# Router scores of four token tiles in one product, with the router's weights stationary and the tokens moving

## The chip, the core and the metric

The kernel runs on one core of one Trainium2 chip. A core has five engines that work in parallel, each through its own queue of instructions in order: PE (TensorE, matrix products), DVE (VectorE), ACT (ScalarE), POOL (GpSimd) and SP (SyncE, here only for issuing transfers). Products land in PSUM, which has eight banks; everything else lies in SBUF. The metric is the device time of one execution in microseconds (us), and the time of a kernel is the median of its runs.

## The reference

The input is x, 4 batches of 512 tokens with 512 features. A conditioning stage makes hidden rows, and a mixture of 32 experts is applied to them: each token goes to the four experts with the highest router scores, each expert takes at most C = 512 tokens, and what comes later is dropped. Cut to what matters:

```
q_emb  = relu(cond @ W3 + b3)                              # per batch
hidden = relu(((n*x + sum_over_tokens(x)) * q_emb) @ W2 + b2)
h      = rmsnorm(hidden) * norm_w
scores = softmax(h @ gate_w.T)                             # 2048 tokens x 32 experts
w, ids = top_k(scores, 4);  w = w / sum(w)
# place of a token in its expert = number of earlier (token, expert) pairs of the same expert
routed = sum over the four experts of  w * (silu(g) * u) @ w2[e],  g, u = split(h @ w13[e])
shared = (silu(h @ shared_gate) * (h @ shared_up)) @ shared_down
out    = x + hidden + routed + shared
```

All of it is in f32.

## The kernel before

The 2048 tokens are 16 tiles of 128 (NT = 16); four tiles make a batch of the input and also a group for the router's bookkeeping (TB = 4). The kernel has three stages. The first, the token stage, takes the tiles one after another and ends with a table that says which token stands in which slot of which expert. The second is a loop over blocks of expert work, which gathers rows, multiplies them with the weights of two experts at once (in two column tiles of PE, 64 columns each) and scatters the results. The third sums up. The change is in the first.

Each step t of the loop at L818 writes instructions for several tiles at different points of their way. The order in which the calls stand in the code is the order in each engine's queue; semaphores are derived from reads and writes, cell by cell in SBUF and by whole bank in PSUM. The calls of one step are, in order:

- `hidden(t)` (L591): four products of 128x512 into a bank D (PE); DVE adds b2; ACT applies relu, the square with its sum, and the root.
- `logits(t - 2)` (L641): router scores of one tile. The tile's tokens, hT of 128x128 per chunk of features, are the stationary operand, and the router's weights gateT (128x32 per chunk) move. The bank is TX[1] or TA[1] in turn.
- `prefix(g)` (L695): five small products that count earlier pairs, in step i = 1 of a group.
- `h_transpose(t - 1)` (L629): PE turns h of the tile before into bank TA[0], ACT copies it to hT (DVE in the last step).
- `slots` (L793): products of one-hots, two tiles in each of steps i = 0 and i = 1 of the group after.
- `top4(t - 2)` (L648): DVE takes the maximum of a tile's scores, subtracts it, and ranks them (max, max_index).
- `first`: one piece of the group's bookkeeping, given by i: `taken`, `places`, `one_hots`, `one_hots`.
- `normed(t)` (L608): DVE takes the reciprocal and makes h; SP sends h to DRAM.
- `rest`: the second piece of the same: `totals`, `places2`, and `one_hots` of another tile.
- For i = 1, 2 of a batch: `z_mean` (ACT) and `z_finish` (POOL) for the next batch's input z, two chunks of features per step.
- `transfers`: larger loads, among them `load_xt(2)` at t = 4 and `load_xt(3)` at t = 8, which fill the z of batches 2 and 3. They stand in SP's queue behind that step's h.

Group and step come from `g, i = divmod(t - 5, TB)` (L820), so the group of tiles 0 to 3 has its `taken` at t = 5. In `one_hots` (L789) the place one-hots are made by ACT for even tiles and by DVE for odd ones, four per tile; the block one-hots (L780) are four DVE instructions of 128x128 per tile. Group 2 has only i = 0 and 1 in the loop; the rest of it and group 3 follow after the loop (from L908 on), in an order written out by hand, together with the shared expert's first products, the tables, and the first gathers.

Of the kernel before, what the change touches and what calls it, by code (L numbers as in the profile page):

```python
# [6 lines left out]
F32 = mybir.dt.float32  # L7
# [4 lines left out]
ALU = mybir.AluOpType  # L12
AX = mybir.AxisListType

P = 128
EPS = 1e-6

LEAST_EXPONENT = -87.33655
# [6 lines left out]
class Program:  # L25
# [87 lines left out]
    def op(self, eng, fn, r=(), w=(), lane=None, signal=True, also=(), key=None):  # L113
        need = {}

        def depend(token):
            key, val = token
            need[key] = max(need.get(key, 0), val)

        for token in also:  # L120
            depend(token)
        for x in r:
            for c in self.cells(x):
                if c in self.writer:
                    t = self.writer[c]
                    if not (eng == "PE" and self.owner[t[0]] == "PE"):
                        depend(t)
        for x in w:
            for c in self.cells(x):
                if c in self.writer:  # L130
                    t = self.writer[c]
                    if not (eng == "PE" and self.owner[t[0]] == "PE"):
                        depend(t)
                for t in self.readers.get(c, {}).items():
                    if not (eng == "PE" and self.owner[t[0]] == "PE"):
                        depend(t)
        if lane is not None:
            ring = self.lanes[lane]
            key = ring[self.lane_next[lane]]
            self.lane_next[lane] = (self.lane_next[lane] + 1) % len(ring)  # L140
            if self.count[key]:
                depend((key, self.count[key]))
            self.count[key] += 16
            token, step = (key, self.count[key]), 16
        elif signal:
            key = key or self.own[eng]
            self.count[key] += 1
            token, step = (key, self.count[key]), 1
        else:
            token, step = None, 0  # L150
        waits = self.learn(eng, need)
        if token:
            self.seen[token] = dict(self.known[eng])
            for x in r:
                for c in self.cells(x):
                    self.readers.setdefault(c, {})[token[0]] = token[1]
            for x in w:
                for c in self.cells(x):
                    self.writer[c] = token
                    self.readers.pop(c, None)  # L160
        else:
            assert not w
        self.out[eng].append((waits, fn, token and token[0], step))
        return token
# [43 lines left out]
def adaln_moe_kernel(nc, stack, x, xt, cond, W3, b3, W2, b2, norm_w, gate_w, wx, sg, su, sd, out):  # L208
    B, S, H = x.shape
    Q = cond.shape[1]  # L210
    E = gate_w.shape[0]
# [4 lines left out]
    NT = T // P  # L216
    TB = S // P
    HC = H // P
# [22 lines left out]
    op = k.op  # L241
# [10 lines left out]
    def keep(name, shape, dtype):  # L252
        n = SIZE[dtype]
        for s in shape[1:]:
            n *= s
        t = k.sbuf(name, shape, dtype, top[0])
        top[0] += -(-n // 32) * 32
        return t

    hid0 = keep("hid0", [P, TB, H], F32)  # L260
    hT = [keep(f"hT{b}", [P, HC, S], F32) for b in range(B)]
    ident = keep("ident", [P, P], F32)
# [4 lines left out]
    xT = [keep(f"xT{i}", [P, HC, P], F32) for i in range(2)]  # L267
# [7 lines left out]
    last = keep("last", [P, 2, NCOL], F32)  # L275
# [10 lines left out]
    gateT = keep("gateT", [P, HC, E], F32)  # L286
# [4 lines left out]
    iota_lo = keep("iota_lo", [P, P], F16)  # L291
    iota_bk = keep("iota_bk", [P, 2, NCOL], F16)
    tok = keep("tok", [P, NT], F32)
# [12 lines left out]
    lg = keep("lg", [P, NT, E], F32)  # L306
    topv = keep("topv", [P, NT, 8], F32)
    topr = [keep(f"topr{i}", [P, 8], F32) for i in range(2)]
# [3 lines left out]
    GROUPS = [(t, t + TB) for t in range(0, NT, TB)]  # L312
# [60 lines left out]
    def instead(name, shape, dtype, of):  # L373
        return k.sbuf(name, shape, dtype, k.place[of.name][1])
# [3 lines left out]
    kept = instead("kept", [P, NT, E], F32, rows[2])  # L378
    W3_sb = instead("W3_sb", [P, QC, H], F32, eo[0])
    sq = instead("sq", [P, H], F32, eo[2])  # L380
    within = instead("within", [P, NT, E], F16, eo[3])


# [11 lines left out]
    TX = [k.bank(f"TX{i}", i) for i in range(2)]  # L395
    GU = [k.bank(f"GU{i}", 2 + i) for i in range(2)]
    TA = [k.bank(f"TA{i}", 4 + i) for i in range(2)]
# [99 lines left out]
    def dve_scalar(o, i, s1, s2, *ops):  # L497
        op("DVE", lambda e: e.tensor_scalar(o, i, s1, s2, *ops), r=[i], w=[o])
# [39 lines left out]
    def transposes(pairs):  # L538
        def fn(e):
            for o, i, n in pairs:  # L540
                last = e.transpose(o, i, ident[:n, :n])  # L541
            return last
        return fn
# [27 lines left out]
    for c in range(QC):  # L571
        op("PE", transposes([(TA[0][:, c * 8 : c * 8 + B], cond_sb[:, c * P : (c + 1) * P], B)]),
           r=[cond_sb[:], ident[:]], w=[TA[0][:]])
# [4 lines left out]
    for c in range(HC):  # L578
        bank = (TX + GU)[c]
        op("PE", matmuls([(bank[:, 0:B], W3_sb[:, kc, c * P : (c + 1) * P], condT[:, kc, :]) for kc in range(QC)]),  # L580
           r=[W3_sb[:], condT[:]], w=[bank[:]])
# [59 lines left out]
    def logits(t):  # L641
        b, j = divmod(t, TB)
        bank = logit_bank(t)
        pl = bank[:, 0:E]
        op("PE", matmuls([(pl, hT[b][:, c, j * P : (j + 1) * P], gateT[:, c, :]) for c in range(HC)]),
           r=[("hT", t), gateT[:]], w=[bank[:]])

    def top4(t):  # L648
        bank = logit_bank(t)
        pl = bank[:, 0:E]  # L650
        l, tr = lg[:, t, :], topr[t % 2][:]

        op("DVE", lambda e: e.max(tr, pl), r=[bank[:]], w=[tr])
        op("DVE", lambda e: e.tensor_scalar(l, pl, tr[:, 0:1], LEAST_EXPONENT, ALU.subtract, ALU.max),
           r=[bank[:], tr], w=[l])
        tv, ti = topv[:, t, :], ids[:, t, :]
        op("DVE", lambda e: e.max(tv, l), r=[l], w=[tv])
        op("DVE", lambda e: e.max_index(ti, tv, l), r=[l, tv], w=[ti])


    def count(o, i):
# [118 lines left out]
    def block_hots(g, t):  # L780

        i = t - GROUPS[g][0]
        e1, bh = ej[g % 2][:, i, :], blh[t % 4]
        for n in range(K):
            op("DVE", lambda e, n=n: e.tensor_scalar(bh[:, n, :], iota_lo[:], e1[:, n : n + 1], tok[:, t : t + 1],
                                                     ALU.is_equal, ALU.mult),
               r=[iota_lo[:], e1, tok[:]], w=[bh[:, n, :]])

# [4 lines left out]
    def slots(t):  # L793

        lh, bh = loh[t % 4], blh[t % 4]

        def fn(e):
            for n in range(K):
                last = e.matmul(GU[1][:, 0:P], lhsT=bh[:, n, :], rhs=lh[:, n, :], start=(t == 0 and n == 0),
                                stop=(t == NT - 1 and n == K - 1))  # L800
            return last
        op("PE", fn, r=[lh[:], bh[:]], w=[GU[1][:]])
# [14 lines left out]
                 13: lambda: fetch(4)}  # L817
    for t in range(NT):  # L818

        g, i = divmod(t - 5, TB)  # L820
        first, rest = [], []
        if g in (0, 1) or g == 2 and i < 2:
            u = GROUPS[g][0] + 2 * (i - 2)
            first, rest = [([lambda: taken(g)], [lambda: totals(g)]),
                           ([lambda: places(g)], [lambda: places2(g)]),
                           ([lambda: one_hots(g, u)], [lambda: one_hots(g, u + 1)]),
                           ([lambda: one_hots(g, u)], [lambda: one_hots(g, u + 1)])][i]
        hidden(t)
        if t == 1:
            gate_transpose()  # L830
        if t >= 2:
            logits(t - 2)
        if g in (0, 1, 2) and i == 1:
            prefix(g)
        if t >= 1:
            h_transpose(t - 1, "ACT" if t < NT - 1 else "DVE")
        if g in (1, 2) and i in (0, 1):
            for u in (0, 1):
                slots(GROUPS[g - 1][0] + 2 * i + u)

        if t >= 2:
            top4(t - 2)
        for fn in first:
            fn()
        normed(t)
        for fn in rest:
            fn()
        if t == 0:
            constants()
        b, i = divmod(t, TB)  # L850
        if b + 1 < B and i in (1, 2):
            for c in (2 * i - 2, 2 * i - 1):
                z_mean(b + 1, c)
                z_finish(b + 1, c)
        if t >= TB:
            sum_rows(t)
        if t in transfers:
            transfers[t]()
# [55 lines left out]
    for e in range(FREE):  # L914
# [22 lines left out]
       r=[cumj[:], ones[:]], w=[TA[1][:]])  # L937
# [6 lines left out]
       w=[active[:]])  # L944
# [4 lines left out]
       r=[ranks[:], before[:], till[:], active[:]], w=[TA[1][:]])  # L949
    op("PE", matmuls([(TA[0][0:1, 4 * NCOL : 4 * NCOL + E], active[:, i : i + 1], upto[:]) for i in range(2)]),  # L950
       r=[active[:], upto[:]], w=[TA[0][:]])
# [13 lines left out]
    for i in range(2):  # L965
        op("DVE", lambda e, i=i: e.tensor_scalar(place[i][:], iota_bk[:], rank[:, i : i + 1], None, ALU.is_equal),
           r=[iota_bk[:], rank[:]], w=[place[i][:]])
    op("DVE", lambda e: e.tensor_tensor(places12[:], place[0][:], place[1][:], ALU.add), r=[place[0][:], place[1][:]],
       w=[places12[:]])
    for t in (12, 13):  # L970
# [9 lines left out]
       r=[scol[:], units], w=[TA[0][:]])  # L980
    op("PE", lambda e: e.matmul(TA[0][0:1, 2 * NCOL : 4 * NCOL], lhsT=ecol[:], rhs=units, start=True, stop=True),
       r=[ecol[:], units], w=[TA[0][:]])
# [21 lines left out]
    for t in range(12, NT):  # L1004
# [11 lines left out]
       r=[empty[:], spare[:], GU[0][:]], w=[idxf[:]])  # L1016
# [14 lines left out]
       r=[needs[:]], w=[tab[:]])  # L1031
# [6 lines left out]
       w=[rel[:]])  # L1038
# [294 lines left out]
    for b in order:  # L1333
# [8 lines left out]
       w=[copies[:]])  # L1342
# [4 lines left out]
    for j in (1, 2, 3, 0):  # L1347
# [4 lines left out]
       r=[copies[:], lrow[0][:], lrow[1][:]], w=[GU[1][:]])  # L1352
# [89 lines left out]
```

## Time and profile before

| | |
|---|---|
| median of 3 runs | 560.28 us (560.17 to 561.66) |
| the profiled execution: its own time | 562.46 us |
| its span in the profile | 560.6 us |
| granted clock of PE over the span | 0.997 |
| PE busy | 549.7 us (98%) |
| DVE busy | 287.2 us (51%) |
| ACT busy | 220.8 us (39%) |
| POOL busy | 287.4 us (51%) |
| start of the expert loop | 121.65 us |
| 12 of the 16 router products (logits) on PE, in the chain | 0.81 us each |
| 64 block one-hots on DVE | 15.6 us busy |

The rows of the profile are times in us from the start of the span unless marked ns. An engine's busy time is a sum over the whole span and can hide that the engine is full in one stage. The chain of waits follows the work that ended last back to the start, at each step to what released it. PE's matmuls are pipelined: a row's duration runs to its last result, so two rows in a row overlap, and the spacing of their starts is what PE really needs. The product of two f32 operands appears as two records.

### The profile page before, as it was taken

To read this page: it belongs to the slowest core of one execution; us is meant where nothing else is said; L and a number is where in the kernel's file an instruction comes from. 1 tells how busy PE (TensorE), PEld (TensorE's weight loads), DVE (VectorE), ACT (ScalarE), POOL (GpSimd) and SP (SyncE) were. 2 spreads that over 40 slices of the span, in tenths; PEclk is the share of its full clock that TensorE was granted. 3 is DMA by queue.
4 is the path that set the end of the run, shared out by engine and by line. 5 is a ranking of instruction groups with operands and counts; after the bars stand their busy time and mean duration, and the time that the engine had idled before them with its cause. 6 is when DMAs were issued, how large, how long until landed. Compare 5 with 4: busy or idle time off the path is not lost.

```text
span 560.6 us, 7813 instructions
## 1 busy us (share of the span) xinstructions
PE 549.7 (98%) x2518; PEld 237.1 (42%) x2518; DVE 287.2 (51%) x807; ACT 220.8 (39%) x428; POOL 287.4 (51%) x237
## 2 busy tenths in 40 slices
PE   8999999999999999999999999999999999989997
PEld 5455665443433333433334433334333334334342
DVE  3569998956455444555444554444554445210422
ACT  3648666823334433434333344333344334300000
POOL 1102200235766666576667776756766766415800
PEclk9999999999999999999999999999999999989999
DMA  8886888956686968797997889989999655439921
GB/s 300 286 324 239 283 337 279 360 174 190 111 198 112 238 147 197 197 238 180 250 260 185 236 242 267 238 230 251 222 250 248 113 103 92 67 56 381 343 77 75
DMA packets 49198, 120.21 MB, mean 214 GB/s; under 512 B 8404, under 2 KB 9432, under 8 KB 48056
## 3 DMA queue, kind: packets, MB, share of 16 engines
q1 hardware_dynamic: 32896, 83.24, 43.9%
q0 software_dynamic: 15040, 34.39, 31.2%
q10 hardware_dynamic: 1208, 1.92, 1.0%
q8 instruction: 26, 0.43, 0.3%
q14 instruction: 28, 0.23, 0.1%
HBM read 89.36 MB, written 34.36 MB: 221 GB/s over the span
## 4 chain that ended last, share of the span: by engine, by line
PE 92%; DVE 3%; ACT 2%; issue 1%; DMA 1%; POOL 0%; SPq 0%; DVEq 0%; ACTq 0%
PE GU L1157 37%; PE D L1180 20%; PE D L548 7%; PE TX L541 5%; PE TX L548 5%; PE GU L548 4%; PE TA L541 4%; PE D L1319 2%; PE TA L1319 2%; PE TX L880 2%; PE TA L548 1%; DMA z<-in_xt_dram 1%; PE D L598 1%; PE D L558 1%; PE D L1312 1%
## 5 line engine op out<-in xcount | busy, mean ns | idle before, releaser
L1108 POOL DMA_INDIRECT y_rows<-eo,sidx x122 | 180.4, 1479 | 102.8 <-DMA y_rows<-eo,sidx 34.7
L1157 PE MATMUL GU<-ring,xT 128*64 x488 | 214.5, 592 | 0.6 <-issue 0.6
L1157 PE MATMUL GU<-up,xT 128*64 128x512 f32 x488 | 214.5, 592 | 0.0
L1157 PEld LDWEIGHTS GU<-ring,xT 128*64 128x64 f32 x488 | 66.8, 137 | 139.4 <-issue 139.4
L1165 DVE TENSOR_TENSOR act<-silu,GU 128x256 f32<-128x256 f32 x61 | 25.7, 422 | 176.3 <-ACT silu L1164 143.4
L1180 PE MATMUL D<-ring,actT 128*64 x244 | 111.3, 599 | 0.2 <-issue 0.2
L1180 PE MATMUL D<-down,actT 128*64 128x512 f32 x244 | 111.3, 599 | 0.0
L1100 POOL DMA_INDIRECT rows<-h_rows,idx x66 | 70.5, 1068 | 33.6 <-issue 13.1
L1164 ACT ACTIVATE silu<-GU 128x256 f32<-128x256 f32 x61 | 23.5, 385 | 147.6 <-PE GU L1157 147.6
L1157 PEld LDWEIGHTS GU<-up,xT 128*64 128x64 f32 x488 | 66.8, 137 | 0.0
L1068 ACT COPY up<-ring 128x1024 f32 x62 | 64.3, 1037 | 5.8 <-DVE up L1068 5.5
L1184 ACT ACTIVATE eo<-D,wrow 128x512 f32<-128x512 f32 x61 | 41.9, 687 | 51.5 <-PE D L1180 42.7
L1180 PEld LDWEIGHTS D<-ring,actT 128*64 128x64 f32 x244 | 30.9, 136 | 58.0 <-issue 58.0
L548 PE MATMUL D<-W_sb,z 128*128 128x512 f32 x120 | 54.3, 595 | 0.2 <-POOL z L563 0.2
L1068 DVE COPY up<-ring 128x1024 f32 x62 | 44.7, 721 | 0.8 <-issue 0.8
L1068 DVE COPY down<-ring 128x1024 f32 x62 | 42.7, 714 | 0.1
L1096 DVE COPY xT<-TX 128x512 f32<-128x512 f32 x62 | 40.0, 686 | 4.4 <-issue 2.0
L563 POOL TENSOR_SCALAR z<-z,vs,q_sb 128x512 f32<-128x512 f32 x12 | 9.8, 816 | 55.7 <-ACT junk L554 55.6
L541 PE MATMUL TX<-ident,rows 128*128 128x128 f32 x248 | 32.3, 273 | 0.0
L1171 ACT COPY actT<-TA 128x256 f32<-128x256 f32 x61 | 22.8, 373 | 24.1 <-PE TA L541 18.1
L548 PEld LDWEIGHTS D<-W_sb,z 128*128 128x128 f32 x120 | 21.7, 190 | 22.4 <-issue 22.0
L1180 PEld LDWEIGHTS D<-down,actT 128*64 128x64 f32 x244 | 30.9, 136 | 0.0
(207 smaller groups left out, 561.2 us busy)
## 6 DMA issues: line engine op xcount, KB each, us to landing
ring<-in_L_ffn_w_dram SPq DMA_DIRECT2D x96, 384.0 KB
ring<-in_L_ffn_w_dram SPq DMA_DIRECT2D x8, 1536.0 KB
y<-y_rows SPq DMA_DIRECT2D x8, 1024.0 KB, 13.4
h_rows<-h SPq DMA_DIRECT2D x16, 256.0 KB, 4.5
y_rows<-hid SPq DMA_DIRECT2D x16, 256.0 KB, 4.1
out_dram<-y SPq DMA_DIRECT2D x16, 256.0 KB, 2.3
z<-in_xt_dram SPq DMA_DIRECT2D x14, 256.0 KB, 5.3
y_rows<-eo,sidx POOLq DMA_INDIRECT x122
```

The costliest lines, as they stand in the source:

```text
L541: last = e.transpose(o, i, ident[:n, :n])
L548: last = e.matmul(o, lhsT=lt, rhs=rh, start=(n == 0), stop=(n == len(terms) - 1))
L1068: return e.copy(dst, src) if eng == "ACT" else e.tensor_copy(dst, src)
L1096: return op("DVE", lambda e: e.tensor_copy(xt[:], pt[:].rearrange("p (c t) -> p c t", c=HC)), r=[pt[:]], w=[xt[:]])
L1100: op("POOL", lambda e: e.indirect_dma_start(out=r[:], out_offset=None, in_=h_dram, in_offset=bass.IndirectOffsetOnAxis(ap=idx[:, i : i + 1 ...
L1108: op("POOL", lambda e, o=o, y=y, at=at: e.indirect_dma_start(out=y, out_offset=bass.IndirectOffsetOnAxis(ap=at, axis=0), in_=o, in_offset= ...
L1157: last = e.matmul(pg[h * U : (h + 1) * U, :], lhsT=xt[:, c, h * U : (h + 1) * U], rhs=w, start=(c == 0), stop=(c == HC - 1))
L1164: op("ACT", lambda e: e.activation(s, pg[:, 0:I], AF.Silu), r=[pg[:]], w=[s])
L1165: op("DVE", lambda e: e.tensor_tensor(a, s, pg[:, I : 2 * I], ALU.mult), r=[s, pg[:]], w=[a])
L1171: op("ACT", lambda e: e.copy(at[:], pt[:, 0 : IC * P].rearrange("p (c t) -> p c t", c=IC)), r=[pt[:]], w=[at[:]])
L1180: last = e.matmul(po[h * U : (h + 1) * U, :], lhsT=at[:, c, h * U : (h + 1) * U], rhs=w2, start=(c == 0), stop=(c == IC - 1))
L1184: op("ACT", lambda e: e.activation(o, po[:], AF.Copy, scale=w), r=[po[:], w], w=[o])
```

## The change

The scores of a group of four tiles are made in one go when its fourth tile is ready, at t = 5, 9 and 13. In `group_logits` the router's weights are the stationary operand, 32 columns wide, and the tokens move, 128 at a time; the four tiles of the group go to the four column tiles of PE, that is to partitions 0 to 31, 32 to 63 and so on of one bank, with the chunks of features as the outer loop. The result stands with experts in the partitions. DVE copies it to SBUF (lgT), PE turns it back (`group_back`), and DVE takes maximum, subtraction and lower bound for all four tiles at once (`group_top4`), and then ranks each tile as before (`rank_tile`). The last group keeps the old form.

The block one-hots of groups 0 and 1, eight tiles, are made by POOL instead of DVE. The bookkeeping of each group is one step later (`t - 6`). lgT lies in the place of xT[0], which is first used later.

```diff
+    lgT = instead("lgT", [P, P], F32, xT[0])
...
         op("DVE", lambda e: e.tensor_scalar(l, pl, tr[:, 0:1], LEAST_EXPONENT, ALU.subtract, ALU.max),
            r=[bank[:], tr], w=[l])
+        rank_tile(t)
+
+    def rank_tile(t):
+        l = lg[:, t, :]
         tv, ti = topv[:, t, :], ids[:, t, :]
         op("DVE", lambda e: e.max(tv, l), r=[l], w=[tv])
         op("DVE", lambda e: e.max_index(ti, tv, l), r=[l, tv], w=[ti])
+
+    def group_logits(g):
+        bank, ht = TA[1], hT[g]
+        def fn(e):
+            for c in range(HC):
+                for q in range(TB):
+                    last = e.matmul(bank[q * E : (q + 1) * E, 0:P], lhsT=gateT[:, c, :], rhs=ht[:, c, q * P : (q + 1) * P],
+                                    start=(c == 0), stop=(c == HC - 1))
+            return last
+        op("PE", fn, r=[gateT[:]] + [("hT", g * TB + q) for q in range(TB)], w=[bank[:]])
+        op("DVE", lambda e: e.tensor_copy(lgT[:], bank[:, 0:P]), r=[bank[:]], w=[lgT[:]])
+
+    def group_back():
+        op("PE", transposes([(TX[1][:, 0:P], lgT[:], P)]), r=[lgT[:], ident[:]], w=[TX[1][:]])
+
+    def group_top4(g):
+        pl = TX[1][:, 0:P].rearrange("p (t e) -> p t e", t=TB)
+        t0, t1 = GROUPS[g]
+        l, tr = lg[:, t0:t1, :], topr[g % 2][:, 0:TB]
+        op("DVE", lambda e: e.tensor_reduce(tr, pl, AX.X, ALU.max), r=[TX[1][:]], w=[tr])
+        op("DVE", lambda e: e.tensor_tensor(l, pl, tr.unsqueeze(2).to_broadcast([P, TB, E]), ALU.subtract),
+           r=[TX[1][:], tr], w=[l])
+        dve_scalar(l, l, LEAST_EXPONENT, None, ALU.max)
+        for t in range(t0, t1):
+            rank_tile(t)
...
-            op("DVE", lambda e, n=n: e.tensor_scalar(bh[:, n, :], iota_lo[:], e1[:, n : n + 1], tok[:, t : t + 1],
+            op("POOL" if g < 2 else "DVE", lambda e, n=n: e.tensor_scalar(bh[:, n, :], iota_lo[:], e1[:, n : n + 1], tok[:, t : t + 1],
                                                      ALU.is_equal, ALU.mult),
...
-        g, i = divmod(t - 5, TB)
+        g, i = divmod(t - 6, TB)
...
-        if t >= 2:
+        if t >= NT - TB + 2:
             logits(t - 2)
+        if t >= TB and t % TB == 1:
+            group_logits(t // TB - 1)
         if g in (0, 1, 2) and i == 1:
             prefix(g)
...
-        if t >= 2:
+        if t >= TB and t % TB == 1:
+            group_back()
+        if t >= NT - TB + 2:
             top4(t - 2)
+        if t >= TB and t % TB == 1:
+            group_top4(t // TB - 1)
         for fn in first:
             fn()
         normed(t)
```

## The prediction

> **What bounds the kernel now.** I read the page, then the table of stages, the chain of waits, and the timelines of DVE, ACT, POOL and PE over the first 125 us. The change touches only the token stage, which ends where the expert loop begins, at 121.6 us.
>
> ```profile
> 48.30:68.50 20.20, 20.17 (x102) 12.50 (x103) 19.47 (x76) 14.82 (x39) 3.47 (x4) 1.00 0.84 283
> 68.50:93.70 25.20, 25.18 (x130) 15.80 (x129) 22.76 (x93) 15.42 (x36) 0.00 (x0) 1.00 0.84 301
> 93.70:121.60 27.90, 26.55 (x115) 12.63 (x114) 23.27 (x84) 17.72 (x44) 10.53 (x13) 1.00 0.82 288
> 121.60:560.00 438.40, 431.89 (x2002) 169.56 (x2002) 194.22 (x461) 148.93 (x251) 265.58 (x199) 1.00 0.75 194
> ```
>
> The columns are the stretch, its length, and the busy us of PE, PEld, DVE, ACT and POOL. From 48.3 to 68.5 DVE is busy 19.47 of 20.20 us beside a PE that never stops: time taken from one is not yet time won. The expert loop is PE-bound, so it only moves with its start.
>
> ```profile
> 35.25 0.76 DVE h L611
> ...
> 36.95 5.33 DMA z<-in_xt_dram
> 42.30 0.73 ACT junk L554 x2
> ...
> 46.63 1.65 POOL z L563 x2
> 48.28 0.04 issue
> 48.33 3.70 PE D L548 x8
> 52.03 0.81 PE TX L548 x8
> 52.84 0.47 PE TA L541 x4
> ...
> 92.75 0.91 PE TA L548 x8
> 93.66 0.02 issue
> 93.68 0.21 DVE topr L653
> ```
>
> This is the chain (start, us, what). Two places matter. At 48.33 hidden(8) starts on a loaded z: the load is issued behind h(4), then come ACT's means and POOL's z_finish; PE's own work up to there is not on the chain. At 93.68 the chain passes to DVE, in top4(15); from there DVE runs almost without a gap to 112.
>
> **The change, part by part.**
>
> *PE.* Twelve logits products of 0.81 us go. Three group products and three turns back come. The nearest row to a group product is the expert loop's:
>
> ```profile
> 129.82 0.38 PE L541 MATMUL TA<-ident,act 128*128 128x128 f32 x2
> 130.43 0.64 PE L1180 MATMUL D<-ring,actT 128*64 x1 [0.23 <-issue]
> 130.44 0.64 PE L1180 MATMUL D<-down,actT 128*64 128x512 f32 x1
> 130.91 0.59 PE L1180 MATMUL D<-ring,actT 128*64 x1
> ```
>
> Two column tiles start 0.01 us apart and take 0.43 us a record of 512 columns, with two records a product: they run side by side. A 128-column product is then 2 x 0.43/4 = 0.215 us; sixteen of them take 0.86 us four abreast, 1.7 two abreast, 3.44 in a row. The same rows show an idle 0.23 us at the switch from the full array to column tiles; leaving them and the last record's tail (0.16 beyond its spacing) add about 0.35. [...] The row gives the drain its price: 0.86 + 0.23 + 0.35 = 1.45 us per group product (bounds 1.1 and 4.0). [...] The router's weights are in fact loaded for each of the four column positions; the short load (a 64-column load is 0.14 us and hides) costs nothing while the previous product streams. The turn back is a transpose, 0.11 us in a row of others, 0.25 with its wait for the lgT copy, which runs while PE turns h (0.47). If DVE is late, hidden(t+1) behind it in PE's queue is late by as much. Per group: 4 x 0.81 = 3.24 out, 1.70 in, 1.5 us won, three times 4.6.
>
> *DVE.* Four top4 took 0.95 each from start to start, 3.8. In their place: the lgT copy 0.25 (the gateT copy is 0.28), a reduction 0.31 (csum 0.36, wsum 0.28), a subtraction 0.30 (sel 0.27), a maximum 0.2 (between 0.14, a quarter of DVE's z_finish, and 0.28, within), four rankings at 0.42: 2.75. Won 1.05 per group; each of these small estimates is good to 0.1. The 32 block one-hots that leave DVE were 0.96 per tile, 7.7 us in all.
>
> *POOL.* No one-hot on POOL is in the trace. The same form is z_finish, 0.82 us for 512 f32 elements: a quarter, 0.20, is the low end, all of it the high end. iota_lo of the same shape took 0.24, a 128x128 tensor_tensor 0.43; I take 0.31. Sixteen start when places2 ends, so 5 us of POOL work stand in its queue ahead of z_finish for batch 3 (not due for 10 us) and ahead of slots two steps later. At 0.31 that is hidden; the cover is gone above 0.8.
>
> [...] The row:
>
> ```profile
> 46.98 0.55 DVE L737 SCALAR_TENSOR_TENSOR lo<-blk,ppc 128x16 f32<-128x16 f32 x1
> ...
> 46.63 1.64 POOL L563 TENSOR_SCALAR z<-z,vs,q_sb 128x512 f32<-128x512 f32 x2 [1.92 <-ACT junk L554]
> ```
>
> That DVE instruction takes 0.17 elsewhere; under POOL's it waited until the first of the two had ended. [...] Since starts fall anywhere, I take 0.4 us at the start of hidden(12); low end 0.
>
> *What moves.* Each group's steps come one tile later (t - 6). For group 2, places and places2 move from t = 14 to t = 15, ahead of h(15) and top4(14) on DVE. SP's issues keep their order.
>
> **The sum, walked step by step.** PE needs 3.44 for hidden and 0.47 to turn h.
>
> 1. To hidden(8). hidden(4) needs POOL's z_finish, which ends at 28.61: it starts at 28.65, was 28.95. So h(4), the load and everything behind it move by 0.3. PE has 1.5 us more than it needs, and waits: hidden(8) at 48.05, was 48.33. The first group's win is lost there, up to 0.3.
> 2. To hidden(12). PE: 4 x 3.91, a group product and turn back 1.70, prefix 0.22, two slots 0.45 each: 66.5. But ACT now makes the place one-hots of tile 2 (1.85 us) at t = 9, ahead of the means of batch 3. hid(9) comes at 55.65, its relu, square and root end at 58.05, hT(8) 58.55, one-hots 60.4, two means 62.1, the same of tile 10 and hT(9) 64.5, two means 66.0, z_finish 67.0. hidden(12) starts at 67.0, 67.4 with the port; it was 68.47.
> 3. To top4(15). The turn back of group 2 is at hidden(12) + 3.44 + 0.47 + 3.44 + 1.45 + 0.45 + 0.25 = +9.5. From there DVE has no gap: group_top4 2.5, h(13) 0.9, place one-hots 0.65, hid(14) 0.65, top4(12) 0.95, taken 2.0, h(14) 0.9, totals 0.5, hid(15) 0.65, a wait of 0.4 for PE's turn, hT(14) 0.6, top4(13) 0.95, places 1.6, h(15) 0.85, places2 0.85, top4(14) 0.95, block one-hots 0.95: 16.9. So top4(15) is at hidden(12) + 26.4; it was +25.2. The late shift takes 1.2 back. At 67.4 + 26.4 = 93.8 it stands at 0.1 past the old 93.68.
> 4. idf, behind it, took 0.65 instead of 0.17 to 0.29 under POOL's product of the weights; ACT's exp now comes some 0.6 earlier, so about 0.25 of that stall goes.
>
> Sum: -0.15 us on the span. From top4(15) on, DVE's work is the same and back to back, and PE follows it. The sum is made against the profiled execution (span 560.6, its own time 562.46, 1.9 outside the span); I carry the difference to the median, 560.28, which is 2.2 below that execution: 560.1. Both kernels should have the same 1.9 outside. A difference under 0.3%, 1.7 us, is about what a measurement of this kernel cannot tell from no change.
>
> **The rivals.**
>
> *The stage follows PE alone (faster).* If loads and ACT kept ahead and DVE's slack held, 4.6 us would come through, 555.7; with half of it, 558. For it: PE shows no gap from 24 to 88. Against it: the chain at 48.33 does not go through PE, and step 3 is DVE's. Chance 0.18, 555.5 to 558.6.
>
> *POOL and DVE take each other's turns (slower).* One place: from the end of places2 (50.85), while POOL works off sixteen one-hots. [...] For it: the stretched lo, and a form of one-hot that was never on POOL. Against it: DVE has about 2 us of room at t = 8. Chance 0.28; 561.9 to 566.
>
> *The product does not do what it says (slower).* If the four column tiles run in a row, 2.5 us come on top at t = 13, uncovered, and 2.1 at t = 9 (the other 0.5 hides behind z): 564.7. Against it are the two halves 0.01 us apart. Chance 0.04. Two abreast, 0.85 more each time, stays within the range.
>
> **How the numbers follow.** Likeliest, 0.50: a balance, 558.6 to 561.9, with 560.1 as its number. Faster 0.18, slower 0.28 + 0.04 = 0.32. The range 557.2 to 563.0 takes in half of each side case and leaves out about 0.2.
>
> **What would show it.** Right: hidden(8) within 0.5 us of 48.1 and waiting for z; hidden(12) near 67.4; sixteen one-hots of about 0.31 each on POOL in a row after places2; the group product near 1.45 us with its tiles starting together; top4(15) near 93.8, DVE full from group_top4 of group 2 on; expert loop from about 121.5. Wrong: the loop starting before 120 or after 123.3; hidden(12) still on a chain of PE alone; one-hots over 0.45 us, or a stretched h and place one-hots at 54 to 57; sixteen products in a row.

## The result and the profile after

| | before | after |
|---|---|---|
| median, us (7 runs each) | 560.28 (559.92 to 561.66) | 558.84 (558.28 to 559.19) |
| ratio, 95% interval | | 0.9958 [0.9938, 0.9979] |
| span of the profiled execution, its own time | 560.6, 562.46 | 557.0, 558.84 |
| hidden(4), hidden(8), hidden(12) on PE | 28.95, 48.33, 68.47 | 28.95, 48.38, 68.27 |
| top4(15) on DVE | 93.68 | 94.33 |
| start of the expert loop | 121.65 | 122.26 |
| from there to the end of the span | 438.95 | 434.74 |
| waits and products of PE right behind the loop | 2.21 + 5.40 | 0 + 3.43 |

By the medians the changed kernel is 1.4 us faster, 0.26%, inside the 0.3% that the prediction called no difference. The interval of the ratio leaves out 1, so a small gain is there. The table shows something odd: the stage that was changed ended 0.6 us *later*, and the whole gain of the two profiled executions, 3.6 us of span, lies behind the expert loop, in code that the change did not touch.

The table of stretches of the changed kernel, cut at the same events as before (the columns are again the stretch, its length, and the busy us of PE, PEld, DVE, ACT and POOL):

```profile
48.38:68.27 19.89, 18.46 (x103) 9.58 (x103) 15.72 (x58) 15.69 (x42) 16.94 (x20) 1.00 0.90 301
68.27:94.33 26.06, 24.96 (x145) 14.98 (x146) 20.11 (x85) 13.92 (x33) 13.06 (x16) 1.00 0.87 308
94.33:122.26 27.93, 26.55 (x116) 12.62 (x115) 23.30 (x85) 17.70 (x44) 10.56 (x13) 1.00 0.76 263
122.26:557.00 434.74, 429.92 (x2002) 169.06 (x2002) 193.55 (x461) 148.92 (x251) 266.31 (x199) 1.00 0.76 195
```

From hidden(8) to hidden(12) PE is busy 18.46 us instead of 20.17, and DVE 15.72 instead of 19.47: both were relieved as intended. The stretch became shorter by only 0.25 us (19.89 instead of 20.14). POOL went from 3.47 to 16.94. The chain of waits says who took the place:

```profile
35.36 0.77 DVE h L612
...
36.98 5.42 DMA z<-in_xt_dram
42.42 0.73 ACT junk L555 x2
...
49.61 0.75 DVE h L612
51.27 13.40 POOL blh L818 x16
64.68 3.54 POOL z L564 x4
68.27 3.70 PE D L549 x8
...
75.84 1.01 PE TA L672 x32
...
93.54 0.88 DVE blh L818 x4
```

hidden(8) still hangs on the same load of z. hidden(12), which was on a chain of PE's own work, now hangs on POOL: sixteen block one-hots in 13.40 us, then z_finish, which stood behind them in POOL's queue. What PE gained it spends waiting, as its list of waits shows (us in total, times, longest):

```profile
PE D L549 <- POOL z L564: 3.3, 3, 1.3
PE TA L542 <- DVE h L612: 2.9, 3, 1.3
```

The list of before had 0.2 us for z in one place and nothing for h.

Now the stretch behind the loop. First the chain of before, then that of after; in both, the first row is the last work of the loop's ending and the last row the first eight products after it:

```profile
489.70 3.63 PE TX L548 x8
493.33 2.21 issue
495.54 5.40 PE GU L548 x8
```

```profile
490.29 3.63 PE TX L549 x8
493.92 3.43 PE GU L549 x8
```

"issue" is time in which PE waited for nothing that the profile shows. Between these two places PE jumps: the kernel has one ending for each possible number of blocks (61 were run), and from each a branch goes to the common code behind them. The eight products that follow the standstill also ran slowly. The table of stretches of before has the granted clock as the third column from the right:

```profile
495.50:497.50 2.00, 1.96 (x4) 0.99 (x5) 0.00 (x0) 0.00 (x0) 0.00 (x0) 0.86 0.04 9
497.50:499.50 2.00, 2.00 (x4) 0.69 (x3) 0.00 (x0) 0.00 (x0) 0.00 (x0) 0.50 0.00 0
499.50:501.00 1.50, 1.50 (x6) 0.69 (x5) 0.00 (x0) 0.00 (x0) 0.00 (x0) 0.72 0.00 0
```

So before paid 2.21 us of standstill and 5.40 - 3.43 = 1.97 us in slow products, 4.2 in all, and after paid nothing. By the three rows the clock stood at half for about 3.4 us, from some 1.4 us behind the standstill on, which is 1.7 of the 1.97 us; the other 0.27 came at full clock too (3.70 instead of 3.43 in before_again, below). 4.2 less the stage's 0.6 is the 3.6 us between the spans. The medians differ by 1.4 only, so an ordinary execution of before must pay less than the profiled one. The experiments had to settle two things: whether the standstill has to do with the edit's work at all, and where PE's and DVE's relief went.

### The profile page after: what moved, and what is told of

Read it like the earlier page. It is cut to its first block, busy times and chain, and to the rows that moved or that the text cites. A ratio compares the mean times of both kernels' runs of the same rounds, so it can differ in the third digit from the quotient of the medians.

```text
span 557.0 us, 7816 instructions
## 1 busy us (share of the span) xinstructions
PE 543.0 (97%) x2521; PEld 228.6 (41%) x2521; DVE 276.3 (50%) x763; ACT 220.8 (40%) x428; POOL 314.6 (56%) x269
## 4 chain that ended last, share of the span: by engine, by line
PE 87%; DVE 5%; POOL 3%; ACT 3%; DMA 1%; issue 1%; SPq 0%; ACTq 0%; DVEq 0%
PE GU L1196 38%; PE D L1219 20%; PE TX L542 5%; PE D L549 4%; PE TX L549 4%; PE GU L549 4%; PE TA L542 4%; POOL blh L818 2%; PE D L1358 2%; PE TA L1358 2%; PE TX L919 1%; DMA z<-in_xt_dram 1%; PE D L599 1%; POOL z L564 1%; ACT sq L606 1%; PE D L559 1%
```

## Experiments

### Where the gain is: the place of code behind the loop

The edit puts products into PE's ending for 80 blocks, where they are never executed. Here it is with the eight products of before_tail_moved; before_tail_256 has 128 of them, and after_tail_moved, on the changed kernel, 120:

```diff
             ending(i)
+            if i == NMAX:
+                k.raw("PE", lambda e: [e.matmul(D[1][:, 0:1], lhsT=zero[:, 0:P], rhs=zero[:, 0:1], start=True, stop=True)
+                                       for _ in range(8)])
```

The expectations count two instructions for a product, and that is wrong. In the trace of before a product of f32 operands is two records, each with its own load of weights (60 products of `hidden` at L548: 120 records and 120 loads), which makes four instructions. In the compiled programs the code behind the loop moved by 32 instructions (not 16), 512 (not 256) and 480 (not 240). The edit of this case moved it by 15.

**before_tail_moved.** 

> The kernel before, with eight products that are never executed put into PE's code of the ending for 80 blocks (61 are run), so that PE's code after the expert loop lies 16 instructions further on; all executed work is the same. Theory (the gain of the change is where that code comes to lie: PE stood 2.2 us at the jump behind the expert loop and ran its next eight products in 5.4 us instead of 3.4): no wait of over 0.3 us ahead of these products, 3.4 to 3.7 us for them, expert loop from 121.7 as before, 558.0 to 558.6 us, some 0.5 under the changed kernel. Rival (the stall was an accident of one profiled execution, and the change's gain lies in its own work): 560.3 us, no different from before.

Measured: 559.04 us (22 runs) beside 560.52 of the kernel before (64 runs), ratio 0.9969 [0.9958, 0.998]: 0.4 us above the range of the theory, and clear of the rival. The chain has no standstill:

```profile
489.99 3.63 PE TX L548 x8
493.62 3.43 PE GU L548 x8
```

**before_again**, the kernel before, unchanged. 

> The kernel before, profiled a second time. Theory (its code behind the loop lies badly, and each execution pays some of it): a wait of 0.3 to 2.5 us at or near the first products after the loop, span less loop start 435.5 to 439 us (four other profiles have 434.3 to 434.8, the first one of this kernel 438.95). Rival (an accident of the first profile): no wait, 434.3 to 434.8 us. The start of the expert loop also tells how far two profiles of the same token stage differ: 121.65 the first time, 122.4 in the kernel with the code moved.

Measured: this execution took 559.89 us, its span is 558.1, the loop starts at 121.86. The standstill is there again, shorter, and without the slow products:

```profile
489.61 3.63 PE TX L548 x8
493.24 1.46 issue
494.70 3.70 PE GU L548 x8
```

**before_tail_256.** 

> The kernel before with 128 never executed products in PE's ending for 80 blocks, so that PE's code after the loop lies exactly 256 instructions further on, at the same place modulo 256. [...]

Measured: 561.48 us (12 runs), ratio to before 1.0007 [0.9989, 1.0025], no different from before, beside 559.04 of before_tail_moved. With 512 instructions instead of 32 the standstill is back, and so is the slow clock (0.93 over 480 to 500 us):

```profile
490.07 3.63 PE TX L548 x8
493.70 2.14 issue
495.84 5.40 PE GU L548 x8
```

**after_tail_moved.** 

> The changed kernel, with 120 never executed products in the same place, so that PE's code after the loop lies 240 instructions further on, within one instruction of where the kernel before had it modulo 256. Theory (place of the code): the wait of about 2 us ahead of the first eight products after the loop comes back, they take over 5 us, 560.3 to 563 us, that is 1.5 to 4 more than the changed kernel. Rival (an accident, or the gain is in the work): 558.8 us, no wait there.

Measured: 559.15 us, ratio to before 0.9974 [0.9965, 0.9984]; no standstill (493.13 3.43 directly behind 489.50 3.63). The expectation failed, but the kernel was not where it was meant to be: it lies 15 + 480 = 495 instructions past the place of before, 17 short of the 512 of before_tail_256, instead of 15 + 240 = 255. So this run does not test whether the changed kernel stands still at the place of before.

What follows: a move of 32 instructions, with every executed instruction the same, gives 1.5 us; a move of 512 gives nothing. Counted from the place of before, the standstill is there in all three profiles at 0 and 512 (before, before_again, before_tail_256), and in none of the eleven others, at 15, 32 or 495. So what counts is the place of the code. The traces show transfers of instructions there: the queue q8, which the profile lists as "instruction" and which I take for PE's, moves packets of 16 KiB, 26 in each of the three executions with a standstill against 25 in before_tail_moved and in after. In those three the packet that was under way as the standstill began landed at 494.23, 493.36 and 494.44 us, and PE went on 1.31, 1.34 and 1.40 us later; in the other eleven PE starts these products before the packet under way has landed (in after at 493.92, the packet landing at 494.29). So "issue" here fits a wait for code, whose length would follow from when a packet lands; that is my reading of these times, and no run shows it directly. The number of packets alone does not tell: after_tail_moved has 26 too. Not shown is which place of the code is the bad one and why, nor how often the effect comes back: the runs have it at 0 and 512, and that the place should count modulo 256, as two of the expectations have it, was my assumption.

The edit lengthened PE's code ahead of this point by 15 instructions, and that was enough: 558.84 and 559.15 with the change against 559.04 for before with its code moved.

With that, the stage itself: the loop starts at 121.65, 121.86, 122.39 and 122.25 in the four profiles in which the stage is that of before (mean 122.04), and at 122.26 and 121.83 in the two in which it is that of after (mean 122.05). The 0.6 us between the first two profiles is inside this scatter. The work of the change is worth nothing that can be seen, within about 0.4 us.

### Where the relief went: the parts alone

**before_hots_pool.** Edit, on before_tail_moved:

```diff
-            op("DVE", lambda e, n=n: e.tensor_scalar(bh[:, n, :], iota_lo[:], ...
+            op("POOL" if g < 2 else "DVE", lambda e, n=n: e.tensor_scalar(bh[:, n, :], iota_lo[:], ...
```

> Of the change the POOL part alone: the kernel before, with the code moved by 16 instructions as in the first experiment (its time 559.04 us is the one to compare with), and the block one-hots of the first eight tiles on POOL. Theory (DVE sets the stage, and the 7.7 us that leave it count where a group's steps pile up): expert loop 1 to 3 us earlier than with the code moved alone (122.4), 556 to 558 us. [...]

Measured: 559.35 us, beside 559.04 of before_tail_moved; the loop starts at 121.96. DVE's busy time between 68 and 94 us fell from 23.95 to 20.98, and nothing came of it: with twelve products for the logits PE is busy 25.98 of these 26 us. The theory fell. (PE also stood 1.58 us at the jump into the ending, which was 0.4 to 0.9 in the other profiles but one, where it was 1.36, so part of the 559.35 is not the stage's.)

**after_hots_dve.** Edit, on the changed kernel: the same line back to `op("DVE", ...`. 

> The changed kernel with the block one-hots of all tiles on DVE again. Theory (sixteen one-hots of 0.84 us on POOL hold up z_finish of batch 3, 1.3 us of PE's wait at hidden(12)): z_finish follows ACT's means, hidden(12) at 66.7 to 67.4 instead of 68.3, expert loop from 121.2 to 121.9 instead of 122.3, 558.0 to 558.6 us. Rival (DVE is as full as POOL: 7.7 us of one-hots in its queue delay hid and h, so that hidden(12) waits for the means instead): hidden(12) at 68.0 or later, loop from 122.3 or later, 558.8 to 560 us.

Measured: 563.02 us, ratio 1.0046 [1.0032, 1.006]; hidden(12) at 70.58, loop from 126.55. The theory fell, and the rival's price was too small. POOL's queue is empty, but DVE now holds everything up:

```profile
PE TA L542 <- DVE h L612: 4.9, 6, 1.4
PE D L549 <- POOL z L564: 2.6, 3, 1.1
```

At t = 9 a whole group's ranking, two tiles' block one-hots and one tile's place one-hots stand on DVE between hid(9), at 57.43, and hid(10), at 65.33; in the changed kernel these two are at 56.16 and 61.79. ACT's relu and means, and z_finish, follow hid(10).

**after_one_earlier.** Edit, on the changed kernel:

```diff
-        g, i = divmod(t - 6, TB)
+        g, i = divmod(t - 5, TB)
```

> The changed kernel with the groups' bookkeeping one tile earlier (t - 5 as before, instead of t - 6), one-hots still on POOL. Theory (the late shift of group 2 costs 1.2 us between hidden(12) and top4(15), and one-hots a tile earlier are off POOL before z_finish of batch 3 is due): hidden(12) near 67, top4(15) at hidden(12) + 25, expert loop from 120 to 121, 556.6 to 557.6 us. Rival (ranking and counting of a group in one step of DVE at t = 5, 9 and 13 delay h and so PE): hidden(8) or hidden(12) 1 us or more later than in the changed kernel, loop from 122.3 or later, 558.8 us or more.

Measured: 561.38 us, ratio 1.0019 [1.0009, 1.0028]; hidden(8) at 49.39, hidden(12) at 70.39, loop from 124.70. The rival was right: ranking and counting of a group fall into one step, hid(9) stands at 57.38 and hid(10) at 65.08, and PE also waits 2.9 us for mask at the prefix products:

```profile
PE TA L542 <- DVE h L612: 3.0, 5, 1.3
PE GU L549 <- DVE mask L697: 2.9, 3, 1.2
```

What follows: taking the logits together relieves PE but gives DVE the ranking of four tiles at once. With the one-hots left on DVE the loop starts 4.5 us later than in the changed kernel (126.55 against 122.05), and with the bookkeeping left a step earlier 2.65 us later (124.70). The move of the one-hots to POOL and the later step do not gain anything against the kernel before; they keep the gathered ranking from colliding with DVE's other work. The product without either move was not run.

### POOL's price for a one-hot

**after_pool_sizes.** Edit, on the changed kernel: five more tensor_scalar instructions on POOL near the start. 

> The changed kernel with five more POOL instructions at the start, where POOL is idle; their results are not used: the one-hot's form (is_equal, mult, two scalars per partition) at 512 f16 elements, at 64, at 128 with add in place of is_equal, at 128 with one operation and one scalar, and at 128 f32 elements. Theory A (POOL's price is per instruction, 0.84 us for 128 elements beside 0.82 for z_finish's 512): all five 0.75 to 0.9 us. Theory B (the price is per element, and the comparison or f16 is slow): 512 elements 2.5 to 3.4 us, 64 about 0.42, and the form with add or with f32 about 0.2 to 0.3. Theory C (the price is per operation or scalar): the one with one scalar about 0.42.

Measured (timeline of POOL, start, us, what; in the order of the list above):

```profile
2.17 2.09 POOL L546 TENSOR_SCALAR blh<-iota_lo,tok 128x512 f16<-128x512 f16 x1
4.26 0.57 POOL L546 TENSOR_SCALAR blh<-iota_lo,tok 128x64 f16<-128x64 f16 x1
4.82 0.44 POOL L546 TENSOR_SCALAR blh<-iota_lo,tok 128x128 f16<-128x128 f16 x1
5.25 0.59 POOL L546 TENSOR_SCALAR blh<-iota_lo,tok 128x128 f16<-128x128 f16 x1
5.84 0.78 POOL L546 TENSOR_SCALAR lgT<-iota_pp,tok 128x128 f32<-128x128 f32 x1
```

None of the three theories has it alone. The comparison is what is dear: with is_equal and mult the price grows by (2.09 - 0.57) / 448 = 3.4 ns per element on top of about 0.35 us; with add and mult it is 0.44 us at 128 elements and 0.79 at z_finish's 512, about 0.9 ns per element (f16 against f32, so a rough figure). f16 or f32 makes little difference (0.84 in the kernel, 0.78 here). Where I scaled 512 elements of z_finish down to 128, I had the wrong operation and left out the fixed part. This one execution took 561.47 us: its z load took 6.59 us, and hidden(8) came at 50.16.

### What the stage hangs on instead

**after_loads_early.** Edit, on the changed kernel:

```diff
-    3: lambda: fetch(0), 4: lambda: load_xt(2), 6: lambda: fetch(1), 8: lambda: load_xt(3),
+    3: lambda: (load_xt(2), fetch(0)), 6: lambda: fetch(1), 7: lambda: load_xt(3),
```

> The changed kernel with the loads of the third and fourth batch of x issued one tile earlier (at t = 3 and 7, behind the stores of h(3) and h(7), instead of at t = 4 and 8); all computed work is the same. Theory (PE's win is lost because hidden(8) waits for a load that is issued behind h(4), 1.14 us of PE's wait, and that took 4.9 to 6.6 us in three profiles): the load is off the chain, hidden(8) at 47.2 to 47.5 instead of 48.4, hidden(12) 67.0 to 67.6, expert loop 121.0 to 121.5 instead of 122.05, 557.6 to 558.3 us. Rival (the next thing, DVE's ranking in one burst and POOL's one-hots ahead of z_finish, takes the microsecond back): hidden(12) at 68 or later, 558.6 us or more.

Measured: 557.48 us (9 runs), ratio to before 0.9931 [0.991, 0.9952]. hidden(8) at 46.18, hidden(12) at 66.16, loop from 120.15. hidden(4) came 0.8 us earlier in this execution (at 28.11), so distances from it are the fair measure: hidden(8) 18.07 us behind it instead of 19.43, hidden(12) 38.05 instead of 39.32, the loop 92.0 instead of 93.3. The load is off the chain, as the theory had it. POOL's queue still is on it:

```profile
49.43 13.14 POOL L818 TENSOR_SCALAR blh<-iota_lo,ej,tok 128x128 f16<-128x128 f16 x16 [3.31 <-DVE ej L771]
62.56 3.54 POOL L564 TENSOR_SCALAR z<-z,vs,q_sb 128x512 f32<-128x512 f32 x4
```

**after_loads_ranks.** Edit: besides, `rank_tile` of a group's four tiles behind `normed(t)`, and the block one-hots of tile 0 on DVE (`"POOL" if g < 2 and t else "DVE"`). 

> The same with two more moves: the four rankings of a group come behind the normed h of their tile on DVE instead of ahead of it, and the block one-hots of tile 0 stay on DVE, so POOL has twelve of 0.84 us ahead of z_finish instead of sixteen. Theory (the burst of group_top4 holds h back, 2.9 us of PE's waits in three places, and POOL's queue holds hidden(12)): PE's waits for h fall to under 1.5 us in all, hidden(12) at 66.0 to 66.8, expert loop 119.8 to 120.8, 556.4 to 557.4 us. Rival (DVE is full from hidden(12) on, and what is put off comes due later; or hid and ACT's means are the limit): hidden(12) within 0.5 us of the kernel with early loads alone, the same time within 0.5 us.

Measured: 555.89 us (6 runs), ratio to before 0.9908 [0.9878, 0.9938]. hidden(12) at 64.69, 36.68 us behind hidden(4); loop from 118.97. PE still waits 2.4 us for h in two places, so the rankings' part of the theory did not come true.

**after_loads_tile0.** Edit: only the second of these two moves. 

> The changed kernel with the early loads (557.48 us) and only one of the two further moves: the block one-hots of tile 0 stay on DVE, twelve instead of sixteen on POOL ahead of z_finish of batch 4; the rankings stay ahead of h. Theory (POOL's queue of one-hots sets hidden(12): it came 38.05 us after hidden(4) with sixteen, 36.7 with both moves): hidden(12) 36.6 to 37.2 us after hidden(4), 555.9 to 556.6 us. Rival (it was the ranking ahead of h): hidden(12) 37.7 us or more after hidden(4), 557.1 to 557.8 us.

Measured: 556.06 us (6 runs), ratio to before 0.9904 [0.988, 0.9928]. hidden(12) at 65.90, 36.74 us behind hidden(4); waits for h 2.4 us, as with both moves. The loop starts 90.8 us behind hidden(4) instead of 92.0. So it was POOL's queue; the order of the rankings made no difference that can be seen. (The intervals of this run and of after_loads_early overlap, so the distances in the profiles carry this more than the times.) POOL now reaches z_finish before ACT's means:

```profile
50.48 10.23 POOL L818 TENSOR_SCALAR blh<-iota_lo,ej,tok 128x128 f16<-128x128 f16 x12 [3.30 <-DVE ej L771]
60.69 2.02 POOL L564 TENSOR_SCALAR z<-z,vs,q_sb 128x512 f32<-128x512 f32 x2
64.26 1.59 POOL L564 TENSOR_SCALAR z<-z,vs,q_sb 128x512 f32<-128x512 f32 x2 [1.54 <-ACT junk L555]
```

**before_loads_early.** Edit: the early loads in before_tail_moved. 

> The kernel before, with the code moved by 16 instructions (559.04 us) and the loads one tile earlier as in the first of these runs. Theory (its PE is the limit up to hidden(12), it waits 0.2 to 0.5 us at hidden(8), so the early load gives it next to nothing): expert loop 121.4 to 122.1, 558.6 to 559.1 us. Rival (the load pins both kernels alike): 1 us or more, 558.0 or less.

Measured: 558.47 us (22 runs), ratio to before 0.996 [0.9947, 0.9972]; loop from 121.33, hidden(12) 39.55 us behind hidden(4), what it was without (39.52 in the first profile). The theory holds, with a time and a loop start just under its ranges: before, PE's own work filled this stretch.

What follows: PE's relief is real and was locked up. Without the standstill and with the early loads, the old form takes 558.47 and the new form, with twelve one-hots on POOL instead of sixteen, 556.06. Behind hidden(4), hidden(12) comes 2.8 us sooner and the loop 2.0 us. Both kernels in which tile 0's one-hots went back to DVE beat the two kernels of this case; the last 0.2 us between them is not measurable.

## Why the prediction was right, point by point

The number (560.1, measured 558.84) and the kind (no difference beyond 0.3%) came out. The forecast for the work of the change, -0.15 us, is met by the loop's start: 122.05 against 122.04. The number was 1.3 us too high; the standstill, which the prediction had left as a part of both kernels, is worth 1.5 and is all of the gain.

Part of this is luck. Of the signs that were to show the prediction right, the one-hots of 0.31 us, the group product of 1.45 us and hidden(12) near 67.4 did not come, and one sign of being wrong, one-hots over 0.45 us, did. At hidden(12) the sum held two wrong prices, 0.31 us for a block one-hot, measured 0.84, and 0.4 us for DVE's waits under POOL, which did not come. One was too low and one too high, and they offset each other in part.

1. *To hidden(8): 48.05, waiting for z.* It was 48.38 and waited 1.14 us for z. The mechanism held: the load behind h(4) pins it, and after_loads_early took it away. The 0.3 us that hidden(4) was to come sooner did not come; it was at 28.95 in both.
2. *To hidden(12): 67.4.* It was 68.27, and the step that failed is the price of a block one-hot on POOL: I took 0.31 us from z_finish's row, with 0.20 and 0.82 as its ends. Measured: 0.84 in the kernel. The prediction had named the limit (at 0.31 the one-hots are hidden, "the cover is gone above 0.8"), and after_loads_tile0 showed it by shortening that queue. ACT's means came out as forecast: two at 66.0 in the sum, 66.12 in the trace. In after_loads_tile0 z_finish ends 0.87 us behind the last mean, so by this estimate hidden(12) would have stood near 67.0 without the queue, as forecast before the 0.4 us were added. The queue cost some 1.2 us. The 0.4 us that the sum calls the port is shown by no run: under POOL's one-hots four place one-hots on DVE took 0.81 instead of 0.74, and h(8) its usual 0.75.

```profile
54.79 0.75 DVE L612 SCALAR_TENSOR_TENSOR h<-hid,rstd,nw_bc 128x512 f32<-128x512 f32 x1
55.46 0.81 DVE L810 TENSOR_SCALAR loh<-iota_lo,lo 128x128 f16<-128x128 f16 x4
...
65.94 0.18 ACT L555 ACTIVATION_READ_ACCUMULATOR junk<-z 128x1 f32 x1
```

3. *The group product: 1.45 us, and 0.25 for the turn back.* They took 1.01 and about 0.16 in the chain:

```profile
36.46 1.08 PE L672 MATMUL TA<-hT,gateT 128*32 128x128 f32 x32
37.47 0.66 PE L542 MATMUL TA<-ident,h 128*128 128x128 f32 x4
37.96 0.32 PE L542 MATMUL TX<-ident,lgT 128*128 128x128 f32 x1
```

   Thirty-two records in 1.01 us fit four abreast: the 0.86 of the estimate and 0.15 around it. The drain, for which the sum holds 0.23 + 0.35 = 0.58 us, is shown by no run; by this estimate entering and leaving the column tiles cost at most that 0.15.
4. *To top4(15): hidden(12) + 26.4, 93.8.* It was +26.06, 94.33. DVE's part was sized rightly (group_top4 2.5 us as estimated, then one wait, 0.68 us for PE's turn where 0.4 was expected); the 0.34 us less is about what the group product and the turn back were too dear, less that longer wait. So two errors met: 0.9 too early at hidden(12), 0.34 too late behind it.
5. *idf's stall to shrink by 0.25.* It did not: 0.61 us instead of 0.65.
6. *Everything outside and behind the loop's start equal.* This is the step that hid the gain. The chain of before has the 2.21 us of "issue" and the eight slow products in it, and the prediction has no term for them. The change does not touch that code, but it moves its address, and that removed the standstill.

Of the rivals, "the stage follows PE alone" (555.7) is what the early loads and the shorter POOL queue nearly made of it; "POOL and DVE take each other's turns" (561.9 to 566) had the right engine and the right place, but the price at hidden(12) was 1.2 us, and what counted was POOL's queue ahead of z_finish, and not the turns.

## What to carry to other kernels

Compare two profiles by where each stage starts before the totals are explained: here the totals gained what the changed stage did not, and added code that never runs was the control that showed it. An engine's relief is worth time only up to the next thing that was due nearly as late, here a load and a queue on POOL, and it is worth looking for that thing when a good edit gives nothing. Work gathered into one product on PE arrives as a burst on the engine behind it, so look at what else that engine has to do in the same step.

## What the hardware did that I had not expected

- The same code can cost 0 or 1.7 to 4.2 us at one branch, depending on where it lies: 15 or 32 instructions further on took the cost away, 512 brought it back. It varies from execution to execution (1.46, 2.14 and 2.21 us of standstill in the three profiles that have it), and each time PE went on 1.31 to 1.40 us after a packet of the instruction queue q8 had landed.
- PE's granted clock fell after standstills of 2.21 us (before: 0.50 in the row of 497.50 to 499.50) and 2.14 us (before_tail_256: 0.93 over 480 to 500), and eight products took 5.40 us in both; after 1.46 us in before_again (3.70 us for the eight), and after 1.58 us in before_hots_pool, it stayed at 1.00 over the same 20 us. In before it fell only when the products had run again for about 1.4 us. What sets it off is not shown.
- DVE was held up much under some POOL instructions and little under others: four DVE place one-hots took 0.74 us alone (in after_hots_dve, from 55.89), 0.81 under POOL's block one-hots (in after, from 55.46), and 1.56 under two z_finish (in after_hots_dve, from 62.96 beside 62.88 on POOL). Under the block one-hots h took 0.75 us in the changed kernel, but 0.97 in after_one_earlier. Why is not shown.
- On POOL a comparison with a multiplication took 0.78 to 0.84 us for 128 elements, as long as z_finish's 512 elements (0.79 to 0.82); an addition with a multiplication took 0.44 for 128.
